# Keeping the scan rounds of a four-layer vision network in their written order on each engine

## The chip, the cores and the metric

The kernel runs on one core of one Trainium2 chip. The metric is the device time of one execution in microseconds, the median of several. A profile of one execution stands beside it; its span, from the first instruction to the last, is a little shorter than the device time (13,481.9 us against 13,525.9 us here).

The engines are called by the names of the profile: PE (TensorE, matmuls), PEld (its weight loads), DVE (VectorE), ACT (ScalarE), POOL (GpSimd) and SP (SyncE, which issues nearly all DMAs here). Each takes its own instructions from a queue.

## What is computed

The input is four images of 56 x 56 positions with 96 channels. Layers 0 and 1 are state-space blocks: normalisation, a projection to 192 inner channels, a selective scan over the 3136 positions in four directions (rows, rows reversed, columns, columns reversed), a gate, an output projection; layer 0 adds a two-matrix feed-forward stage, layer 1 convolutions, a fusion and a normalisation. Layers 2 and 3 are linear attention and a feed-forward stage quantised to 8-bit floats. Most of the work is the selective scan, for each image, direction, channel `d` and each of 16 states `n`:

```
dt = softplus(dt_raw @ dtw + dtb)
step:  h[d, n] = exp(dt[d] * A[d, n]) * h[d, n] + dt[d] * B[n] * u[d]
       y[d]    = sum over n of h[d, n] * C[n]
result y + u * D, the four directions added up
```

It is a recurrence along the positions, with 192 x 16 = 3072 independent rows per image and direction.

## The kernel before

**Tiling of the scan.** Each image and direction is cut into 7 chunks of 448 positions. Two layers, four images, four directions and 7 chunks give 224 chunks. A chunk is worked in 8 rounds, `r = 4 e + q`: `e` is the half of the channels (2 x 96), `q` one of four groups of four states. A round holds 3 groups `g` of 128 rows (32 channels x 4 states) by 448 positions. There are 1792 rounds, and `scans()` writes them one after the other, in a software pipeline laid out by hand.

**One round, n**, and the lines that make it:

- L475, PE: `b(n)`, the B values of the round spread over 128 rows, a matmul with a selection matrix into the one PSUM buffer `b`. It takes two instructions in the profile.
- L550, DVE: `v[:, g] = du * b` for g = 0, 1 (and 2 in rounds 5 and 6 of a chunk, the constant `OWN`).
- L522, POOL: in the other rounds `v[:, 2] = du * cb`, from a copy of B that a DMA has spread (`cb`). The code calls this `ahead`. The tile `v` has 3 buffers.
- L513, ACT: the decays `da = exp(dt * a)`, one for each g, into 3 PSUM buffers.
- L556, DVE: the scans, one for each g: `v` becomes the states h.
- L560, ACT: the last column is kept in `carry` for the next chunk of the same direction.
- L566, POOL: `hc = v * C` over all three groups (2 buffers).
- L581, PE, in `add_up`: the sum over the states, four matmuls (8 instructions) into the PSUM tile `y`. After the fourth round of a half, L590 or L592 adds `u * D` or the directions so far, and L593 (ACT) copies the sum into `Y`.

**Written order.** The loop over rounds writes: the products of L550 for round n; then `begin(n + 1)`, which holds `b(n + 1)` and POOL's product of L522 for n + 1; then the three scans of n, each followed by the decay of n + 1 for the same g; the carry copy; `hc` of n; and last `add_up` of n - 1. So on PE `b(n + 1)` is written ahead of the sum of n - 1, and on POOL the product of L522 for n + 1 is written ahead of `hc` of n.

**What feeds the rounds.** In rounds 3 to 7 and at round 0 of a chunk the loop also writes the preparation of the chunk that follows (of the second half at round 0): `project_step` (L413 on PE, L419 or L421 on ACT give `cf`; a DMA writes it to memory as `cd`), `step_sizes` (L433 on PE, softplus L436 on ACT gives `dtc`), `times_u` (L446 on POOL gives `duc`), `spread` (8 DMAs that fetch `dt` and `du`, spread over 128 rows, with 2 buffers each) and `fetch` (4 DMAs that fetch `cb` for one q, 6 buffers).

**The other stages.** At each step of the rounds' generator `tile_net` also draws steps from the stages of another image: `load`, `middle` (the end of layer 0 and the start of layer 1) or `tail` (the end of layer 1, layers 2 and 3), at a pace set by `lengths`. The last `tail` comes after the rounds. Their instructions, such as L620 and L614 (normalisation), L677 (convolution) and L823, go to the same queues.

**What sets the order.** The program isn't run in the order in which it is written. A scheduler plays it through with estimated durations, and on each engine takes the earliest-written instruction that is ready at that moment. The order it finds is the order of each engine's queue on the chip; the durations on the chip differ from its estimates. In the kernel before this holds for all instructions, the rounds' too.

Of the kernel before, what the change touches and what calls it, by code (L numbers as in the profile page):

```python
# [15 lines left out]
AF = mybir.ActivationFunctionType  # L16
ALU = mybir.AluOpType
# [5 lines left out]
C = 96  # L23
# [3 lines left out]
NG = 3  # L27
# [5 lines left out]
CS = 448  # L33
# [121 lines left out]
class Net:  # L155
# [227 lines left out]
    def in_order(self, a, orient, lo, n):  # L383

        a = a.rearrange("p (h w) -> p w h" if orient else "p (h w) -> p h w", w=HS)
        return a[:, lo // HS : (lo + n) // HS, :]

    def project_step(self, ch):

        nc, sp = self.nc, self.sp  # L390
        l, i, k = ch.l, ch.i, ch.k
        if ch.first:
            for n in range(4):
                a = slice(n * L // 4, (n + 1) * L // 4)
                for e in range(NE):
                    nc.sync.dma_start(self.U[e][:, a], self.ud[i][C * e : C * e + C, a])
        if ch.step == 0:
            wd = sp.tile([128, WD], F32, name="wd")
            nc.sync.dma_start(wd, self.aps["wd"][l, k])
            a = NE * 128  # L400
            self.wx = wd[:C, :a].rearrange("p (e m) -> p e m", e=NE)
            self.wt = wd[:, a : a + C]
            a += C
            self.dtb = wd[:C, a : a + NE]
            na = sp.tile([128, NE, NQ, NG], F32, name="na")
            nc.scalar.activation(na.rearrange("p e q g -> p (e q g)"), wd[:, a + NE :], AF.Exp)
            nc.gpsimd.tensor_scalar_mul(na, na, -1.0)
            self.na = na
            self.carry = sp.tile([128, NE, NQ, NG], F32, name="carry")
        ch.na, ch.carry, ch.wt, ch.dtb = self.na, self.carry, self.wt, self.dtb  # L410
        ps = self.ps()[:, :CS]
        for e in range(NE):
            nc.tensor.matmul(  # L413
                ps.rearrange("p (a b) -> p a b", b=HS), self.wx[:, e],
                self.in_order(self.U[e], ch.orient, ch.c * CS, CS), start=e == 0, stop=e == NE - 1,
            )
        ch.cf = sp.tile([128, CS], F32, name="cf")
        if l == 0:
            nc.scalar.activation(ch.cf, ps, AF.Copy, scale=self.cscale[:, k : k + 1])  # L419
        else:  # L420
            nc.scalar.copy(ch.cf, ps)  # L421
        ch.cd = self.dram.tile([2 * NS, CS], F32, tag="cd", name="cd", bufs=3)
        nc.sync.dma_start(ch.cd, ch.cf[: 2 * NS])
# [48 lines left out]
    def spread_b(self, ch, q):  # L472

        ps = self.psum.tile([128, 512], F32, tag="b", name="b", bufs=1)[:, :CS]
        self.nc.tensor.matmul(ps, self.sel[:, q], ch.cf, start=True, stop=True)  # L475
        return ps

    def scans(self):

        nc, sp = self.nc, self.sp
        chunks = []
        for l in range(2):
            for i in range(NB):
                for n, (orient, rev) in enumerate(ORDER):
                    for step in range(NCS):
                        ch = Step()
                        ch.l, ch.i, ch.orient, ch.rev, ch.step = l, i, orient, rev, step  # L490
                        ch.k = 2 * orient + rev if l == 0 else orient + 2 * rev
                        ch.c = NCS - 1 - step if rev else step
                        ch.first = n == 0 and step == 0
                        ch.skip = n == 0
                        ch.last = n == 3 and step == NCS - 1
                        ch.dt, ch.du, ch.cb = [], [], []
                        chunks.append(ch)
        ch = chunks[0]
        self.project_step(ch)
        self.step_sizes(ch)  # L500
        self.times_u(ch, 0)
        self.spread(ch, 0)
        self.times_u(ch, 1)
        for q in range(3):
            self.fetch(ch, q)
        rounds = [(ch, e, q) for ch in chunks for e in range(NE) for q in range(NQ)]
        nexts = dict(zip(chunks, chunks[1:]))

        def decay(n, g):

            ch, e, q = rounds[n]
            da = self.psum.tile([128, 512], F32, tag="da", name="da", bufs=3)[:, :CS]
            nc.scalar.activation(da, ch.dt[e][:, g], AF.Exp, scale=ch.na[:, e, q, g : g + 1])  # L513
            return da

        def begin(n):
            ch, e, q = rounds[n]
            b = self.spread_b(ch, q)
            v = sp.tile([128, NG, CS], F32, name="v", bufs=3)
            ahead = NQ * e + q not in OWN  # L520
            if ahead:
                nc.gpsimd.tensor_tensor(v[:, 2], ch.du[e][:, 2], ch.cb[q][:, 1], ALU.mult)  # L522
            return b, v, ahead

        nxt = begin(0)
        das = [decay(0, g) for g in range(NG)]
        late = None
        for n, (ch, e, q) in enumerate(rounds):
            r = NQ * e + q
            follow = nexts.get(ch)  # L530
            if r == 0:
                self.spread(ch, 1)
                self.fetch(ch, 3)
            if follow is not None:
                if r == 3:
                    self.project_step(follow)
                elif r == 4:
                    self.step_sizes(follow)
                    self.times_u(follow, 0)
                elif r == 5:  # L540
                    self.spread(follow, 0)
                    self.times_u(follow, 1)
                if r > 4:
                    self.fetch(follow, r - 5)
            way = slice(None, None, -1) if ch.rev else slice(None)
            end = 0 if ch.rev else CS - 1
            b, v, ahead = nxt
            at = ch.carry[:, e, q]
            for g in range(2 if ahead else 3):
                nc.vector.tensor_tensor(v[:, g], ch.du[e][:, g], b, ALU.mult)  # L550
            more = n + 1 < len(rounds)
            if more:
                nxt = begin(n + 1)
            for g in range(NG):
                da, das[g] = das[g], None
                nc.vector.tensor_tensor_scan(  # L556
                    v[:, g, way], da[:, way], v[:, g, way], at[:, g : g + 1] if ch.step else 0.0, ALU.mult, ALU.add
                )
                if g == 2 and ch.step < NCS - 1:
                    nc.scalar.copy(at.unsqueeze(2), v[:, :, end : end + 1])  # L560
                if more:
                    das[g] = decay(n + 1, g)
                if g < 2:
                    yield ch
            hc = sp.tile([128, NG, CS], F32, name="hc")
            nc.gpsimd.tensor_tensor(hc, v, ch.cb[q][:, 0].unsqueeze(1).to_broadcast([128, NG, CS]), ALU.mult)  # L566
            if late is not None:
                self.add_up(*late)
            late = (ch, e, q, hc)
            yield ch  # L570
        self.add_up(*late)
        yield None

    def add_up(self, ch, e, q, hc):

        nc = self.nc
        if q == 0:
            self.y = self.psum.tile([128, 512], F32, tag="y", name="y", bufs=1)[:, :CS]

        for n, g in enumerate((0, 1, 2, 2)):  # L580
            nc.tensor.matmul(  # L581
                self.y[32 * n : 32 * n + 32], self.four, hc[:, g], start=q == 0 or n == 3, stop=n == 3,
            )
        if q < NQ - 1:
            return
        y = self.in_order(self.Y[e], ch.orient, ch.c * CS, CS)
        o = self.y[:C].rearrange("p (a b) -> p a b", b=HS)
        if ch.skip:
            u = self.in_order(self.U[e], ch.orient, ch.c * CS, CS)
            nc.tensor.matmul(o, self.skip[ch.l][:, e], u, start=False, stop=True)  # L590
        else:
            nc.tensor.matmul(o, self.ident[:C, :C], y, start=False, stop=True)  # L592
        nc.scalar.copy(y, o)  # L593
        if ch.last:
            nc.sync.dma_start(self.yd[ch.i][C * e : C * e + C], self.Y[e])

# [428 lines left out]
```

## Time and profile before

| | before |
|---|---|
| device time, median of 3 (lowest to highest) | 13,525.92 us (13,524.19 to 13,527.72) |
| span of the profiled execution | 13,481.9 us |
| mean granted TensorE clock | 0.686 |
| end of the last scan | 12,879 us after the start |
| L556 scans on DVE | 5376, 5836.6 us busy |
| L550 products on DVE | 4032, 2329.5 us busy |
| L566 `hc` on POOL | 1792, 5427.9 us busy |
| L522 products on POOL | 1344, 1514.0 us busy |
| L513 decays on ACT | 5376, 3351.7 us busy |

The page gives busy time of each engine, then groups of instructions with the idle time before them and what ended it. An entry such as "DVE v L556 <- POOL v L522" in the list of waits reads: DVE stood idle ahead of an instruction of line 556 that writes `v`, until POOL's instruction of line 522 had ended; then the total in us, the number of waits and the longest. The timeline lists start and duration in us, engine, line, operation, tiles (out<-in), shapes and a count of merged instructions; the bracket at the end is the idle time of the engine just before, and what ended it.

### The profile page before, as it was taken

What the parts mean: (1) busy time and instruction counts of PE and PEld (TensorE: products, weight loads), DVE (VectorE), ACT (ScalarE), POOL (GpSimd) and SP (SyncE); (2) the same over time, 40 slices, a digit from 0 to 9 for tenths busy, and PEclk for the clock granted to TensorE, in tenths of its full rate; (3) what the DMA queues carried; (4) which work ended last, traced back from release to release, by engine and by line L of the source; (5) the groups of instructions that cost most, each with busy time, mean ns of one, the idle gap of its engine ahead of it and who ended that gap; (6) DMA issues with size and microseconds to landing.
All of it is one profiled execution on the core that took longest, in us unless ns stands there. A gap on an engine that the chain in (4) does not pass through costs nothing. (4 is left out here: it accounts for less than half of the span.)

```text
span 13481.9 us, 111978 instructions
## 1 busy us (share of the span) xinstructions
PE 9753.7 (72%) x30078; PEld 3150.5 (23%) x30078; DVE 8491.7 (63%) x10556; ACT 6039.2 (45%) x10401; POOL 7754.4 (58%) x3960
## 2 busy tenths in 40 slices
PE   6677677776777777776777777776777777777776
PEld 2221122211222122211222132211322212222133
DVE  4666766667666766667666655677556675566722
ACT  4544455444544455444554433344333453343511
POOL 4666665666666665666666645557545575555720
PEclk6766666766767676777767676666766667666665
DMA  4444444445444444445444433344334444343410
GB/s 120 118 111 118 117 118 112 111 108 129 115 107 113 116 119 110 112 109 132 115 108 108 114 94 93 90 107 122 95 82 99 96 120 100 89 97 88 118 45 26
DMA packets 940544, 1415.74 MB, mean 105 GB/s; under 512 B 175042, under 2 KB 926148, under 8 KB 938276
## 3 DMA queue, kind: packets, MB, share of 16 engines
q1 hardware_dynamic: 939136, 1406.79, 42.6%
q8 instruction: 237, 3.88, 0.1%
q14 instruction: 399, 3.27, 0.1%
q10 hardware_dynamic: 772, 1.80, 0.0%
HBM read 1139.85 MB, written 268.14 MB: 104 GB/s over the span
## 5 line engine op out<-in xcount | busy, mean ns | idle before, releaser
L566 POOL TENSOR_TENSOR hc<-v,cb 128x1344 f32<-128x1344 f32 x1792 | 5427.9, 3029 | 3097.5 <-DVE v L556 2569.8
L556 DVE TENSOR_TENSOR_SCAN v<-da,carry,v 128x448 f32<-128x448 f32 x4608 | 5042.5, 1134 | 1093.6 <-POOL v L522 821.5
L513 ACT ACTIVATE da<-dt,na 128x448 f32<-128x448 f32 x5376 | 3351.7, 634 | 1959.4 <-DVE v L556 1940.3
L581 PE MATMUL y<-hc,four 128*32 128x448 f32 x14336 | 2848.2, 776 | 1678.3 <-POOL hc L566 1663.9
L475 PE MATMUL b<-cf,sel 128*128 128x448 f32 x3584 | 2673.7, 841 | 1296.7 <-DVE v L550 1294.1
L550 DVE TENSOR_TENSOR v<-du,b 128x448 f32<-128x448 f32 x4032 | 2329.5, 605 | 1640.2 <-PE b L475 1463.7
L522 POOL TENSOR_TENSOR v<-du,cb 128x448 f32<-128x448 f32 x1344 | 1514.0, 1134 | 116.4 <-DMA cb<-cd 77.7
L475 PEld LDWEIGHTS b<-cf,sel 128*128 128x128 f32 x3584 | 830.3, 270 | 3079.5 <-DVE v L550 2464.0
L581 PEld LDWEIGHTS y<-hc,four 128*32 128x32 f32 x14336 | 374.1, 126 | 3756.3 <-POOL hc L566 3089.2
L446 POOL TENSOR_TENSOR duc<-dtc,U 96x448 f32<-96x448 f32 x448 | 552.5, 1244 | 1152.2 <-ACT dtc L436 1090.7
L560 ACT COPY carry<-v 128x3 f32<-128x3 f32 x1536 | 296.4, 193 | 1553.7 <-DVE v L556 1551.0
L593 ACT COPY Y<-y 96x448 f32<-96x448 f32 x448 | 340.0, 759 | 1442.0 <-PE y L592 1104.1
L617 POOL TENSOR_TENSOR rs<-rs,power 112x4 f32<-112x4 f32 x252 | 256.9, 1020 | 1248.3 <-ACT rs L616 1110.7
L556 DVE TENSOR_TENSOR_SCAN v<-da,v 128x448 f32<-128x448 f32 x768 | 794.1, 1073 | 176.5 <-POOL v L522 116.7
L413 PE MATMUL ps<-U,wd 96*128 96x448 f32 x896 | 667.9, 873 | 1.0 <-ACT h L877 0.9
L620 PE MATMUL ps<-ident,rs 112*96 112x112 f32 x2016 | 395.0, 364 | 317.0 <-POOL rs L617 316.7
L592 PE MATMUL y<-Y,ident 96*96 96x448 f32 x672 | 603.1, 990 | 0.0
L677 PE MATMUL ps<-win,dg 64*64 64x220 f32 (+10 forms) x2016 | 591.2, 491 | 0.0
L513 ACT ACT_TABLE_LOAD x432 | 554.3, 1283 | 10.5 <-DMA dt<-dd 3.3
L436 ACT ACT_TABLE_LOAD x313 | 401.6, 1283 | 174.5 <-PE ps L433 100.2
L620 PEld LDWEIGHTS ps<-ident,rs 112*96 112x96 f32 x2016 | 332.1, 242 | 458.2 <-POOL rs L617 435.3
L614 PEld LDWEIGHTS ps<-avg,w 96*112 96x112 f32 (+1 forms) x2240 | 354.6, 232 | 221.8 <-issue 95.3
(207 smaller groups left out, 5804.7 us busy)
## 6 DMA issues: line engine op xcount, KB each, us to landing
cb<-cd SPq DMA_DIRECT2D x3584, 112.0 KB, 3.9
dt<-dd SPq DMA_DIRECT2D x1792, 168.0 KB, 3.5
du<-dd SPq DMA_DIRECT2D x1792, 168.0 KB, 4.4
dd<-dtc SPq DMA_DIRECT2D x448, 168.0 KB, 2.1
dd<-duc SPq DMA_DIRECT2D x448, 168.0 KB, 2.2
U<-u SPq DMA_DIRECT2D x64, 294.0 KB, 6.2
y<-Y SPq DMA_DIRECT2D x16, 1176.0 KB, 6.6
u<-w SPq DMA_DIRECT2D x56, 224.0 KB, 2.8
```

Of the source, the lines that this page charges most:

```text
L413: nc.tensor.matmul(ps.rearrange("p (a b) -> p a b", b=HS), self.wx[:, e], self.in_order(self.U[e], ch.orient, ch.c * CS, CS), start=e == 0 ...
L446: nc.gpsimd.tensor_tensor(du.rearrange("p (a b) -> p a b", b=HS), ch.dtc[e].rearrange("p (a b) -> p a b", b=HS), self.in_order(self.U[e], ...
L475: self.nc.tensor.matmul(ps, self.sel[:, q], ch.cf, start=True, stop=True)
L513: nc.scalar.activation(da, ch.dt[e][:, g], AF.Exp, scale=ch.na[:, e, q, g : g + 1])
L522: nc.gpsimd.tensor_tensor(v[:, 2], ch.du[e][:, 2], ch.cb[q][:, 1], ALU.mult)
L550: nc.vector.tensor_tensor(v[:, g], ch.du[e][:, g], b, ALU.mult)
L556: nc.vector.tensor_tensor_scan(v[:, g, way], da[:, way], v[:, g, way], at[:, g : g + 1] if ch.step else 0.0, ALU.mult, ALU.add)
L566: nc.gpsimd.tensor_tensor(hc, v, ch.cb[q][:, 0].unsqueeze(1).to_broadcast([128, NG, CS]), ALU.mult)
L581: nc.tensor.matmul(self.y[32 * n : 32 * n + 32], self.four, hc[:, g], start=q == 0 or n == 3, stop=n == 3,)
L592: nc.tensor.matmul(o, self.ident[:C, :C], y, start=False, stop=True)
L620: nc.tensor.matmul(ps[:, b], rs[:, q : q + 1].to_broadcast([NT, C]), self.ident[:NT, :NT], start=True, stop=True)
L677: self.nc.tensor.matmul(o[:, a - r0 : e - r0, x0:x1], diag[:, tap], win[:, a + dy - lo : e + dy - lo, x0 + dx : x1 + dx], start=n == 0, st ...
```

## The change

Every instruction of the rounds gets a common mark. Among the instructions that carry it, the scheduler keeps the written order on each engine. Unmarked instructions (the preparation of the next chunk, the DMAs, the other stages) can still be placed anywhere between them. It is meant to make the chip follow the pipeline as it was laid out by hand, where the scheduler's estimates had led it to another order. No operation is added or removed; one operand of L566 is given a name on the way.

```diff
+    def keep(self, i):
+
+        self.tc.stamp_issue_order_token(i.ins, "rounds")
+
...
-        self.nc.tensor.matmul(ps, self.sel[:, q], ch.cf, start=True, stop=True)
+        self.keep(self.nc.tensor.matmul(ps, self.sel[:, q], ch.cf, start=True, stop=True))
...
-            nc.scalar.activation(da, ch.dt[e][:, g], AF.Exp, scale=ch.na[:, e, q, g : g + 1])
+            self.keep(nc.scalar.activation(da, ch.dt[e][:, g], AF.Exp, scale=ch.na[:, e, q, g : g + 1]))
...
-                nc.gpsimd.tensor_tensor(v[:, 2], ch.du[e][:, 2], ch.cb[q][:, 1], ALU.mult)
+                self.keep(nc.gpsimd.tensor_tensor(v[:, 2], ch.du[e][:, 2], ch.cb[q][:, 1], ALU.mult))
...
-                nc.vector.tensor_tensor(v[:, g], ch.du[e][:, g], b, ALU.mult)
+                self.keep(nc.vector.tensor_tensor(v[:, g], ch.du[e][:, g], b, ALU.mult))
...
-                nc.vector.tensor_tensor_scan(
+                self.keep(nc.vector.tensor_tensor_scan(
                     v[:, g, way], da[:, way], v[:, g, way], at[:, g : g + 1] if ch.step else 0.0, ALU.mult, ALU.add
-                )
+                ))
...
-                    nc.scalar.copy(at.unsqueeze(2), v[:, :, end : end + 1])
+                    self.keep(nc.scalar.copy(at.unsqueeze(2), v[:, :, end : end + 1]))
...
-            nc.gpsimd.tensor_tensor(hc, v, ch.cb[q][:, 0].unsqueeze(1).to_broadcast([128, NG, CS]), ALU.mult)
+            c = ch.cb[q][:, 0].unsqueeze(1).to_broadcast([128, NG, CS])
+            self.keep(nc.gpsimd.tensor_tensor(hc, v, c, ALU.mult))
...
-            nc.tensor.matmul(
+            self.keep(nc.tensor.matmul(
                 self.y[32 * n : 32 * n + 32], self.four, hc[:, g], start=q == 0 or n == 3, stop=n == 3,
-            )
+            ))
...
-            nc.tensor.matmul(o, self.skip[ch.l][:, e], u, start=False, stop=True)
+            self.keep(nc.tensor.matmul(o, self.skip[ch.l][:, e], u, start=False, stop=True))
         else:
-            nc.tensor.matmul(o, self.ident[:C, :C], y, start=False, stop=True)
-        nc.scalar.copy(y, o)
+            self.keep(nc.tensor.matmul(o, self.ident[:C, :C], y, start=False, stop=True))
+        self.keep(nc.scalar.copy(y, o))
```

## The prediction

> **What bounds the kernel now.** Part 1 of the page comes first: no engine is full, so waits set the time.
>
> ```profile
> PE 9753.7 (72%) x30078; PEld 3150.5 (23%) x30078; DVE 8491.7 (63%) x10556; ACT 6039.2 (45%) x10401; POOL 7754.4 (58%) x3960
> ```
>
> PE's figure covers modelled, overlapping matmuls. Of the others DVE has most to do, and the rounds give it nearly all of it: lines 550 and 556 (both forms) are 2329.5 + 5042.5 + 794.1 = 8166 us. The scans are serial on DVE, so I ask what ends DVE's idle 13,482 − 8,492 = 4,990 us. The list of waits names two large causes:
>
> ```profile
> DVE v L550 <- PE b L475: 1463.7, 474, 15.1
> DVE v L556 <- POOL v L522: 938.2, 609, 12.0
> ```
>
> I then split DVE's waits by place in the chunk: the k-th scan of line 556 belongs to round k div 3, and likewise for the other lines. Write T for the products of line 550, S for the scans, v2 for POOL's product of line 522, r0 to r7 for the rounds of a chunk. The 938 us lie in r0 to r3. Of the 1,464 us, 807 are T of r1 (164 waits, 4.92 us each) and 215 T of r7 (173 waits, 1.24 each). The other stages' instructions on DVE wait 2,067 us (493 of it after 12,879 us, when no round is left).
>
> The timeline shows how the first cause works, in a stretch without other stages (r1 to r2):
>
> ```profile
> 4592.60 0.59 DVE L550 TENSOR_TENSOR v<-du,b 128x448 f32<-128x448 f32 x1
> 4592.82 3.03 POOL L566 TENSOR_TENSOR hc<-v,cb 128x1344 f32<-128x1344 f32 x1 [1.33 <-DVE v L556]
> 4593.11 2.18 DVE L556 TENSOR_TENSOR_SCAN v<-da,carry,v 128x448 f32<-128x448 f32 x2
> 4593.24 1.86 PE L475 MATMUL b<-cf,sel 128*128 128x448 f32 x2 [1.07 <-DVE v L550]
> 4595.21 0.59 DVE L550 TENSOR_TENSOR v<-du,b 128x448 f32<-128x448 f32 x1
> 4595.81 1.14 POOL L522 TENSOR_TENSOR v<-du,cb 128x448 f32<-128x448 f32 x1
> 4595.90 1.72 PE L581 MATMUL y<-hc,four 128*32 128x448 f32 x8 [0.80 <-POOL hc L566]
> 4596.98 1.15 DVE L556 TENSOR_TENSOR_SCAN v<-da,carry,v 128x448 f32<-128x448 f32 x1 [1.18 <-POOL v L522]
> ```
>
> POOL runs hc of the round before (3.03 us) and only then v2, which this round's third scan needs: DVE stands 1.18 us and POOL then 1.33, so the two take turns. The period is 5.45 us (4596.98 − 4591.53, the same scan a round earlier). A round that waits for nothing takes 4622.94 − 4618.73 = 4.21 us:
>
> ```profile
> 4618.73 1.15 DVE L550 TENSOR_TENSOR v<-du,b 128x448 f32<-128x448 f32 x2 [1.91 <-PE b L475]
> 4619.80 3.23 DVE L556 TENSOR_TENSOR_SCAN v<-da,carry,v 128x448 f32<-128x448 f32 x3
> ...
> 4622.94 1.13 DVE L550 TENSOR_TENSOR v<-du,b 128x448 f32<-128x448 f32 x2
> ```
>
> The second cause, at the start of the same chunk (r0 to r1):
>
> ```profile
> 4576.97 1.72 PE L581 MATMUL y<-hc,four 128*32 128x448 f32 x8
> 4578.62 1.94 PE L592 MATMUL y<-Y,ident 96*96 96x448 f32 x2
> 4580.39 1.28 PE L475 MATMUL b<-cf,sel 128*128 128x448 f32 x2
> 4580.60 0.99 ACT L593 COPY Y<-y 96x448 f32<-96x448 f32 x1 [4.91 <-PE y L592]
> 4581.77 0.62 DVE L550 TENSOR_TENSOR v<-du,b 128x448 f32<-128x448 f32 x1 [4.77 <-PE b L475]
> 4583.61 1.34 POOL L446 TENSOR_TENSOR duc<-dtc,U 96x448 f32<-96x448 f32 x1 [6.21 <-ACT dtc L436]
> 4584.92 1.13 POOL L522 TENSOR_TENSOR v<-du,cb 128x448 f32<-128x448 f32 x1
> 4586.08 1.15 DVE L556 TENSOR_TENSOR_SCAN v<-da,carry,v 128x448 f32<-128x448 f32 x1 [3.69 <-POOL v L522]
> ```
>
> b of r1 stands on PE behind the old chunk's last sum and its identity matmul; ACT holds the new chunk's decays behind that sum's copy; POOL holds v2 of r0 behind duc of the next chunk, which waits for ACT. DVE loses 4.77 + 3.69 us.
>
> **What the Trainium skill says.** "PSUM — Partial Sum Buffer", Engine vs sequencer instructions: the queues of ScalarE, VectorE and GpSimd are strict FIFO, and matmuls start in program order. The trace agrees: v2 waited with its inputs there while duc, ahead of it, stood 6.21 us. "SBUF — State Buffer", Who interferes with whom: a DVE instruction with at most one SBUF input doesn't contend with GpSimd. T reads b from PSUM, S reads da from PSUM, and T takes 582 to 623 ns in all 4,032 cases, whatever POOL does; so running v2 beside other scans costs nothing. "TensorE: Matmul & The Clock Gate", What's actually happening: PE runs at half clock unless it has been busy. The trace shows 0.50 from 4586 to 4604 us and 0.75 from 4623 to 4800. I price PE at half clock.
>
> **The change, part by part.** No operation, buffer or byte is added or removed; only positions in the queues. From the order in the trace I count where before departs from the written order:
> - POOL: v2 starts after the preceding round's hc in 884 of 895 cases of r0 to r3, in none of r4 and r7. Written, v2(n+1) precedes hc(n).
> - PE: b of r1 follows y of r7 in 223 of 223 chunks, b of r7 follows y of r5 in 184. Written, b(n+1) precedes y(n−1).
> - DVE: T(n) slips before the last scan of n−1 in 820 cases, filling the wait for v2. ACT: the copy of Y runs ahead of decays written before it.
>
> New steady state, with S2(n−1) ending at 0. DVE: T to 1.1, scans to 4.2. PE: b(n+1) from 1.2 to 3.1 (1.86 us), then y(n−1), whose hc ends at about 3.2, until 4.9; b(n+2) is wanted at 5.4, so y delays nothing. POOL: hc(n−1) 0.1 to 3.2, v2(n+1) to 4.3, hc(n) at 4.3: 4.17 of work in 4.21. ACT: three decays, 3 × 0.64, each when a scan frees its buffer. So DVE sets 4.21 us, with POOL almost level. The new wait is hc behind v2: if cb or du lands late, hc and y stand too, but the third scan needs that v2 anyway, and in most chunks du and cb land one to three rounds ahead (the median issue of dt is 4 rounds ahead).
>
> The sums, all on DVE's path:
> - A, third scan for v2: 925 us. Of the 672 rounds r1 to r3, 520 take 5.3 to 5.6 us, so 520 × (5.45 − 4.21) = 645 is nearly sure; the rest hangs on r0 and on duc, which stays free to stand ahead of v2, now with a round's slack.
> - B, T of r1 for b: 807 us. b(r1) can start when T of r0 is done; the other stages' matmuls may still stand ahead.
> - C, T of r7 for b: 215 us.
> Together 1,947 us, or 8.7 per chunk. Left as they are: the other T waits for b (1,464 − 807 − 215 = 442, mostly behind convolution matmuls), S for decays (332), du (146), the other stages (2,067).
>
> How much is kept depends on what else a chunk holds. I count 50 chunks without other-stage work (47.8 us each, DVE idle 12.1), 56 with such matmuls alone (52.5, idle 17.3), 118 with other-stage DVE instructions (62.8, idle 23.8, of which 12.5 is these waiting for PE, ACT and POOL). In the first I take 8.5 us, in the second 8. In the last I take half, 4.5: a DVE that comes sooner to an instruction waiting for PE waits there longer. The bounds of that share are 0 and 8.7. Sum: 50 × 8.5 + 56 × 8 + 118 × 4.5 = 1,404; 13,526 − 1,404 = **12,120 us**.
>
> **The rivals.**
> - Only the steady part comes (A's 645): r0 stays held by duc, softplus and other matmuls, which have no order of their own. 12,880 us. For it: PE work sits ahead of b in most chunks. Against: the quiet chunk above stalls with hardly any.
> - More comes: all 1,947, S of r0 for decays (246 of the 332) and half of the 442, since Y's copy no longer blocks ACT. 13,526 − 2,414 = 11,110. Against: the other stages' waits must not grow.
> - Slower: b(n+1), waiting for DVE, now stands ahead of y and of all other-stage matmuls placed behind it; DVE's other-stage instructions wait for those matmuls. They wait 2,067 − 493 = 1,574 us within the scans; if that doubles while only 645 is won, 13,526 + 1,574 − 645 = 14,455; at +65% (1,020), 13,900, which I take. For it: the scheduler had moved these instructions for some reason, and its places for the other stages shift. Against: r4 to r6 mostly keep the written order on POOL and PE and run without these stalls.
> - No change, 13,526: gains eaten exactly.
>
> **How the numbers follow.** Forecast 0.50, steady part alone 0.20, more 0.14, slower 0.13, no change 0.03. Faster is 0.50 + 0.20 + 0.14 = 0.84. The range reaches from the larger gain, 11,100, past the smaller one to 13,200 (that case with the waits of the other stages 20% longer, 315 us); slower and no change stay out, 0.16.
>
> **What would show it.** A: hardly any wait of line 556 for line 522, steady rounds of about 4.2 us. B and C: line 550's wait for b below 600 us, b right behind T in r0. DVE at 69 to 71% of the span with the same busy time. The forecast falls if waits of lines 620, 823 or 834 on DVE grow past 3,000 us, if the wait for v2 remains (duc still ahead), or if line 566 waits for DMA.

## The result, and the profile after

The changed kernel takes 11,818.43 us (median of 4 runs, 11,805.97 to 11,857.94) against 13,525.06 us: a ratio of 0.8744 (95% interval 0.8722 to 0.8766), or 1,707 us less. Adding `keep` shifted the lines: 475 is now 479 (b), 513 is 517 (decays), 522 is 526 (POOL's third product, v2), 550 is 554 (T), 556 is 560 (scans), 566 is 571 (hc), 581 is 586 (the sum y), 592 is 597 (identity).

The busy times of the profile after, part 1 of its page:

```profile
PE 8717.8 (74%) x30078; PEld 2954.7 (25%) x30078; DVE 8442.5 (71%) x10556; ACT 6046.5 (51%) x10428; POOL 7740.7 (65%) x3960
```

DVE, ACT and POOL are busy for nearly the same time as before (ACT has 27 table loads more); the span is 1,626 us shorter (11,856.3), so their shares rise. PE's busy time falls by 1,036 us with the same instructions; more on that at the end. The two waits, from the list of waits:

```profile
DVE v L554 <- PE b L479: 653.3, 277, 11.2
DVE v L560 <- POOL v L526: 534.6, 113, 21.4
```

The first lost more than half, the second somewhat less. Round 3 of a chunk in the timeline after, from its third product on POOL to the products of round 4. In the timelines here, lines of ACT, PEld and DMA are left out, and `...` stands for the other gaps:

```profile
3984.98 1.15 POOL L526 TENSOR_TENSOR v<-du,cb 128x448 f32<-128x448 f32 x1
...
3986.23 1.13 DVE L554 TENSOR_TENSOR v<-du,b 128x448 f32<-128x448 f32 x2
3986.46 3.03 POOL L571 TENSOR_TENSOR hc<-v,cb 128x1344 f32<-128x1344 f32 x1 [0.34 <-DVE v L560]
3987.28 3.23 DVE L560 TENSOR_TENSOR_SCAN v<-da,carry,v 128x448 f32<-128x448 f32 x3
...
3989.44 1.16 POOL L526 TENSOR_TENSOR v<-du,cb 128x448 f32<-128x448 f32 x1
3989.55 1.72 PE L586 MATMUL y<-hc,four 128*32 128x448 f32 x8 [1.11 <-POOL hc L571]
3990.42 1.12 DVE L554 TENSOR_TENSOR v<-du,b 128x448 f32<-128x448 f32 x2
```

The third product of this round ran at 3984.98, ahead of hc of the round before (3986.46), so the three scans run together (3.23 us) and no bracket stands at DVE. The product that starts at 3989.44 is already that of round 4. The round takes 3990.42 − 3986.23 = 4.19 us. A window over rounds 2 to 5 of this chunk shows a full DVE; the columns are the window, its length, and busy time with the number of instructions of each engine, then PE's granted clock, the DMA share and GB/s:

```profile
3982.00:3999.00 17.00, 12.42 (x50) 2.78 (x50) 16.98 (x21) 8.81 (x18) 14.33 (x7) 0.79 0.62 139
```

About half of what is left of the two waits (362 us in round 0 and 224 us in round 2, of 1,188) arises near the start of a chunk:

```profile
3971.42 1.35 POOL L450 TENSOR_TENSOR duc<-dtc,U 96x448 f32<-96x448 f32 x1 [3.40 <-ACT dtc L440]
3972.73 1.13 POOL L526 TENSOR_TENSOR v<-du,cb 128x448 f32<-128x448 f32 x1
3973.81 3.03 POOL L571 TENSOR_TENSOR hc<-v,cb 128x1344 f32<-128x1344 f32 x1
3973.89 1.15 DVE L560 TENSOR_TENSOR_SCAN v<-da,carry,v 128x448 f32<-128x448 f32 x1 [3.03 <-POOL v L526]
...
3976.89 1.72 PE L586 MATMUL y<-hc,four 128*32 128x448 f32 x8 [6.22 <-POOL hc L571]
...
3978.55 1.94 PE L597 MATMUL y<-Y,ident 96*96 96x448 f32 x2
3980.31 1.68 PE L479 MATMUL b<-cf,sel 128*128 128x448 f32 x2
...
3982.02 1.15 DVE L554 TENSOR_TENSOR v<-du,b 128x448 f32<-128x448 f32 x2 [2.79 <-PE b L479]
```

duc of the next chunk, which carries no mark, stands on POOL ahead of v2 of round 0 and waits there for ACT. That costs DVE 3.03 us. Then hc of the old chunk's last round (3973.81) is late too, so are its sum (3976.89) and identity matmul, and b of round 2, now written behind that sum, costs another 2.79 us.

Placing DVE's idle time by round, as in the prediction, gives this table (us, counted in the traces; e1, e2, e7, e9 and e10 are the experiments below). It leaves out the scans' waits for decays, the waits of T for du, and the time after the last scan.

| DVE idle ahead of | before | after | e1 | e2 | e9 | e10 | e7 |
|---|---|---|---|---|---|---|---|
| third scan for v2, rounds 1 to 3 | 733 | 172 | 114 | 678 | 825 | 164 | 59 |
| third scan for v2, round 0 | 193 | 362 | 248 | 187 | 438 | 364 | 68 |
| T of round 1 for b | 807 | 43 | 164 | 218 | 49 | 1,188 | 171 |
| T of round 7 for b | 215 | 18 | 271 | 24 | 15 | 310 | 60 |
| T of round 2 for b | 50 | 224 | 307 | 60 | 16 | 0 | 67 |
| T of the other rounds for b | 392 | 368 | 451 | 421 | 232 | 353 | 386 |
| other stages, while rounds last | 1,580 | 1,332 | 1,345 | 1,388 | 1,435 | 1,278 | 1,314 |

Idle time fell by 1,577 us in all (4,985 to 3,409), which with 49 us less busy is the 1,626 of the span.

### The profile page after: what moved, and what is told of

Read it like the earlier page. It is cut to its first block, busy times and chain, and to the rows that moved or that the text cites. A ratio compares the mean times of both kernels' runs of the same rounds, so it can differ in the third digit from the quotient of the medians.

```text
span 11856.3 us, 112012 instructions
## 1 busy us (share of the span) xinstructions
PE 8717.8 (74%) x30078; PEld 2954.7 (25%) x30078; DVE 8442.5 (71%) x10556; ACT 6046.5 (51%) x10428; POOL 7740.7 (65%) x3960
## 4 chain that ended last, share of the span: by engine, by line
PE 24%; DVE 19%; issue 17%; POOL 10%; DMA 7%; ACT 7%; SPq 3%; DVEq 0%; POOLq 0%; ACTq 0%
DVE v L560 13%; POOL hc L571 6%; DVE v L554 4%; PE y L586 4%; PE ps L682 3%; DMA cb<-cd 3%; PE b L479 3%; SPq L463 2%; PE ps L625 2%; PE ps L417 2%; ACT da L517 2%; PE y L597 2%; DMA du<-dd 2%; POOL v L526 2%; POOL rs L622 1%
## 5 line engine op out<-in xcount | busy, mean ns | idle before, releaser
L560 DVE TENSOR_TENSOR_SCAN v<-da,carry,v 128x448 f32<-128x448 f32 x4608 | 4990.3, 1132 | 720.5 <-POOL v L526 476.5
L586 PE MATMUL y<-hc,four 128*32 128x448 f32 x14336 | 2375.3, 712 | 1240.8 <-POOL hc L571 1193.1
L479 PE MATMUL b<-cf,sel 128*128 128x448 f32 x3584 | 2298.2, 731 | 992.1 <-DVE v L554 989.7
L554 DVE TENSOR_TENSOR v<-du,b 128x448 f32<-128x448 f32 x4032 | 2266.8, 607 | 758.2 <-PE b L479 653.3
L479 PEld LDWEIGHTS b<-cf,sel 128*128 128x128 f32 x3584 | 724.9, 235 | 2612.1 <-DVE v L554 2075.8
L586 PEld LDWEIGHTS y<-hc,four 128*32 128x32 f32 x14336 | 331.2, 121 | 2871.1 <-POOL hc L571 2478.8
L597 PE MATMUL y<-Y,ident 96*96 96x448 f32 x672 | 577.4, 950 | 0.0
```

What stands on the lines that cost most here:

```text
L479: self.keep(self.nc.tensor.matmul(ps, self.sel[:, q], ch.cf, start=True, stop=True))
L554: self.keep(nc.vector.tensor_tensor(v[:, g], ch.du[e][:, g], b, ALU.mult))
L560: self.keep(nc.vector.tensor_tensor_scan(v[:, g, way], da[:, way], v[:, g, way], at[:, g : g + 1] if ch.step else 0.0, ALU.mult, ALU.add))
L586: self.keep(nc.tensor.matmul(self.y[32 * n : 32 * n + 32], self.four, hc[:, g], start=q == 0 or n == 3, stop=n == 3,))
L597: self.keep(nc.tensor.matmul(o, self.ident[:C, :C], y, start=False, stop=True))
```

## The experiments

Ratios are to the kernel before on the same chip, with 95% intervals.

### Which engine's order matters: POOL alone, PE alone, both

The mark is given only on the engines named:

```diff
     def keep(self, i):
-        self.tc.stamp_issue_order_token(i.ins, "rounds")
+        if i.ins.engine in (mybir.EngineType.Pool, ):
+            self.tc.stamp_issue_order_token(i.ins, "rounds")
```

> Only the rounds' POOL instructions keep the written order (the product of line 526 ahead of the preceding round's hc). Theory (each queue's order costs by itself): the third scan's wait for that product in rounds 1 to 3 goes (733 us before), rounds 2 and 3 take about 4.2 us, the wait of T in round 1 for b (807 us) stays: 12,700 to 12,950 us. Rival 1 (the queues are coupled: one engine's order drags the others along): near the full change, 11,800 to 12,000, with the b waits gone too. Rival 2 (POOL's order alone only moves the wait elsewhere): 13,400 or more.

Measured: 12,323.9 us, 0.9116 (0.9099 to 0.9132), 1,198 us less; the theory's window began at 12,700. The waits of the third scan did fall as it said, to 114 us in rounds 1 to 3. But the wait of T in round 1 fell as well, from 807 to 164. The trace shows how: b of round 1 stands behind the old half's sum in 0 chunks here, in 223 before. A likely reason, not shown, is that with hc held behind v2 the scheduler saw the sum ready later and placed b first. So Rival 1 has a part in it: a mark on one queue moved another queue's order. It did not move all of it; b of round 7 is still behind the sum in 194 of 223 chunks (184 before), and T of round 7 waits 271 us for it.

With `mybir.EngineType.PE` in its place:

> Only the rounds' PE instructions keep the written order (b of the next round ahead of y of the round before). Theory (each queue by itself): the waits of T in rounds 1 and 7 for b (1,022 us before) fall below 150, the third scan's wait for POOL stays near 900 us, rounds 1 to 3 stay at 5.45 us: 12,500 to 12,750 us. Rival 1 (coupled): 11,800 to 12,000 with both waits gone. Rival 2 (b ahead of y makes PE stand for DVE, with the other stages behind): slower than before, above 13,600.

Measured: 12,421.1 us, 0.9188 (0.9174 to 0.9203), 1,100 us less. Here only PE changed: v2 still follows hc as before (215 to 223 of 223 chunks in each of rounds 0 to 3), rounds 1 to 3 stay near 5.45 us and the wait for v2 at 865 us in all. The waits of rounds 1 and 7 for b are 242 us together, short of the theory's 150 but 780 below before, and the time is 80 us better than its window. Rival 2, PE standing for DVE with the other stages behind it, falls: the other stages' waits on DVE went down, 1,580 to 1,388.

With both engines:

> POOL and PE keep the written order, DVE and ACT are free. Theory (POOL's and PE's orders are the whole cause; DVE's slipping of T ahead of the last scan was only a filler of the wait for POOL): within 1% of the full change, 11,750 to 11,950 us. Rival (the orders of DVE and ACT matter too, above all the copy of Y ahead of the decays on ACT): 12,100 us or more, with scans waiting for decays as before (332 us).

Measured: 11,930.6 us, 0.8829 (0.8813 to 0.8845). That is 112 us above the full change, just inside 1%, but their intervals lie apart, so the orders of DVE and ACT add something. POOL and PE carry 1,591 of the 1,707 us. Alone they gave 1,198 + 1,100 = 2,298, so they share about 700; e1's effect on b of round 1 is one overlap that the traces show.

### DVE and ACT

The mark is given on the other two engines alone:

> DVE and ACT keep the written order, POOL and PE are free. Theory (POOL's and PE's orders are the whole cause): both large waits stay, 13,300 to 13,650 us, possibly slower than before, since T no longer fills the wait for POOL. Rival (the orders of DVE and ACT carry the gain, or drag POOL and PE into the written order): 12,500 us or less.

Measured: 12,998.2 us, 0.9619 (0.9599 to 0.9638): 523 us less, where the theory had none. The next two runs take them apart: ACT alone (e5), DVE alone (e6).

> Only the rounds' ACT instructions (decays, carry copy, copy of Y) keep the written order. Theory (half of the previous run's unexpected gain of 523 us is ACT: the copy of Y no longer stands ahead of the next chunk's softplus and decays, so duc and with it v2 of round 0 come some 3 us sooner in each chunk): 12,950 to 13,100 us, the wait of T in round 1 for b near 300 us, rounds 2 and 3 still 5.45 us. Rival (the gain was DVE's strict order): 13,400 to 13,600.

Measured: 13,322.9 us, 0.9850 (0.9832 to 0.9869), 199 us less. The theory's mechanism fails: T of round 1 waits 830 us for b, as before. What fell most is the first scan of round 0 waiting for its decays, 246 to 123 us.

> Only the rounds' DVE instructions keep the written order. Theory (T's slipping ahead of the last scan only fills a wait): 13,450 to 13,700 us, no large change in any wait but T of round 1 moved behind the last scan. Rival (strict order on DVE brings the 523 us): 12,950 to 13,100.

Measured: 13,189.9 us, 0.9756 (0.9741 to 0.9770), 332 us less, against the theory. In the 50 chunks that hold no other stage it is right: they take 47.7 us, 47.8 before. The wait of T in round 1 for b only changes its place to the third scan of round 0, which now comes first: 807 + 193 = 1,000 us become 241 + 652 = 893. The chunks with other-stage work are about 1.6 to 1.8 us shorter each, and why is not settled: their instructions may have come to lie better, and PE's mean granted clock is 0.720 here, 0.686 before. In the 50 chunks the clock rose too (0.65 to 0.69) and did not make them shorter.

### Undoing one order inside the full change

All rounds' instructions stay marked; only the place at which one is written moves. First v2 of rounds 0 to 3, behind hc (`third` holds the product that `begin` wrote):

```diff
-            if ahead:
-                self.keep(nc.gpsimd.tensor_tensor(v[:, 2], ch.du[e][:, 2], ch.cb[q][:, 1], ALU.mult))
+            if ahead and (e == 1 or n == 0):
+                third(n, v)
...
             self.keep(nc.gpsimd.tensor_tensor(hc, v, c, ALU.mult))
+            if more and rounds[n + 1][1] == 0:
+                third(n + 1, nxt[1])
```

> All rounds' instructions marked as in the full change, but the third product (POOL) of rounds 0 to 3 is written behind hc of the round before, the order that the kernel before had. Theory (that one inversion makes POOL and DVE take turns): rounds 1 to 3 go back to 5.45 us or a little more, the third scan's wait for POOL rises from 535 us to over 1,000, and the run takes (5.45 - 4.2) x 3 x 224 = 840 us more than the full change: 12,500 to 12,800 us. Rival (the gain in rounds 1 to 3 came from the other queues): within 2% of the full change, below 12,050.

Measured: 12,411.0 us, 0.9186 (0.9168 to 0.9204), 593 us above the full change. The taking of turns is back: the medians of rounds 1 to 3 are 5.46, 5.45 and 5.45 us, and 527 of the 672 take 5.3 to 5.6 us (5 in the full change, 520 before).

```profile
DVE v L564 <- POOL v L531: 1262.9, 735, 21.7
```

This is the wait of the third scan in e9's list of waits, 1,263 us against 535. The time is less than the 840 us I worked out, and below the window. One reason is that the full change pays elsewhere for its order: with hc first, the old half's sum is done sooner, and T of round 2 waits 16 us for b instead of 224, T of the rounds 3 to 6 and 0 waits 232 instead of 368.

Then the sum ahead of b in rounds 1 and 7; the copy of Y, which belongs to the same call, moves ahead with it:

```diff
+            if late is not None and r in (0, 6):
+                self.add_up(*late)
+                late = None
             if more:
                 nxt = begin(n + 1)
```

> All rounds' instructions marked as in the full change, but the sum of two rounds ago is written ahead of b in rounds 1 and 7 (and with it the copy of Y ahead of the decays of round 1), as the kernel before had it. Theory: T of round 1 waits for b again 3 to 4.5 us a chunk, T of round 7 about 1: 700 to 1,000 us on top of the full change, less the 224 us that round 2 waits there: 12,300 to 12,700 us. Rival (with the other orders kept the old half's sum is done in time, so b behind it costs nothing): below 12,000 us.

Measured: 12,932.3 us, 0.9567 (0.9551 to 0.9582), 1,114 us above the full change, more than the theory's window. The timeline of e10 at the start of a chunk (574 is hc, 589 the sum, 600 the identity matmul there):

```profile
4371.06 1.35 POOL L450 TENSOR_TENSOR duc<-dtc,U 96x448 f32<-96x448 f32 x1 [3.74 <-ACT dtc L440]
4372.37 1.12 POOL L526 TENSOR_TENSOR v<-du,cb 128x448 f32<-128x448 f32 x1
4373.46 3.01 POOL L574 TENSOR_TENSOR hc<-v,cb 128x1344 f32<-128x1344 f32 x1
...
4376.52 1.72 PE L589 MATMUL y<-hc,four 128*32 128x448 f32 x8 [8.55 <-POOL hc L574]
...
4378.18 1.94 PE L600 MATMUL y<-Y,ident 96*96 96x448 f32 x2
4379.94 1.63 PE L479 MATMUL b<-cf,sel 128*128 128x448 f32 x2
...
4381.61 1.15 DVE L554 TENSOR_TENSOR v<-du,b 128x448 f32<-128x448 f32 x2 [6.93 <-PE b L479]
```

PE stands 8.55 us for an hc that itself was held behind v2 and duc, and b waits behind it, so T of round 1 loses 6.93 us here. The two orders need each other: v2 ahead of hc makes hc late, and a late hc costs most where b is queued behind its sum.

### What duc still costs

The full change, with the product of line 450 marked as well:

```diff
-        nc.gpsimd.tensor_tensor(
+        self.keep(nc.gpsimd.tensor_tensor(
             du.rearrange("p (a b) -> p a b", b=HS),
...
             ALU.mult,
-        )
+        ))
```

> The full change, and POOL's product duc (line 450) of the next chunk keeps the written order too: after hc of rounds 3 and 4, not ahead of v2 of round 0. Theory (what is left of the third scan's wait in round 0, 362 us, and the new wait of T in round 2 for b, 224 us, come from duc standing on POOL for ACT's softplus): both fall below 100 us, POOL's wait for dtc (1,040 us) nearly vanishes, 11,250 to 11,500 us. Rival (duc then comes too late for the loads of du): T of round 0 waits for the DMA of du for over 400 us (103 us in the full change), 11,800 us or more.

Measured: 11,589.4 us, 0.8571 (0.8559 to 0.8584): the fastest of all, 229 us below the full change. The two waits in its list of waits, over all rounds, are these:

```profile
DVE v L554 <- PE b L479: 682.8, 250, 9.2
DVE v L560 <- POOL v L526: 126.8, 36, 16.8
```

Of them, 68 us are the third scan of round 0 and 67 us T of round 2, both below 100; du lands in time (74 us of waiting), and the chunks without other stages take 37.5 us with 2.8 us of idle DVE, against 40.9 with 5.8. It missed its window because other waits grew: T of round 1 for b by 128 us, scans for decays by 106, and POOL's wait for dtc is still 638 us. The median round 0 takes 4.62 us, 7.33 in the full change and 13.50 before.

> As the run before, and ACT's softplus (line 440) of the next chunk keeps the written order as well, in round 4 behind the decays. Theory (only duc's place matters, softplus ahead of time costs two table loads wherever it stands): within 1% of the run before. Rival 1 (with softplus at round 0 the decays of round 1 come late): faster by over 1%. Rival 2 (softplus just ahead of duc makes POOL wait in round 4, and du lands late): slower by over 1%, with T of round 0 waiting for du.

The edit wraps the softplus of line 440 in `self.keep` too. Measured: 11,727.2 us, 0.8682 (0.8666 to 0.8697), 138 us slower than e7. That is by over 1%, as in Rival 2, but not for its reason: du is waited for 64 us only. T of round 1 waits 422 us for b (171 in e7), and the first scan of round 5 waits 218 us for its decays, behind the softplus.

## Why the prediction was right, and where a size was off

**The mechanism held, engine by engine.** Forecast 12,120 us, range 11,100 to 13,200; measured 11,818. v2 starts behind the preceding hc in no case after (884 of 895 before), b behind the sum in no case. Rounds that wait for nothing take 4.19 us (4.21 forecast). DVE's share is 71%, as forecast; e9 and e10 undo one order each, and its waits come back. T and the scans take as long as before (584 to 623 ns, and 1,114 to 1,152 ns with a carry), so v2 beside the scans cost nothing, as assumed.

**A was too high.** I called 645 us nearly sure, from 520 rounds of 5.45 us. The third scan's wait in rounds 1 to 3 did lose 561 us, but these 520 rounds (each from the end of one last scan to the next) are only 366 us shorter in all, and 322 of them take 4.1 to 4.3 us. Where they are round 2 they gain nothing on average (5.44 to 5.43 us): T of round 2 waits 174 us more for b, and round 0 waits 169 us more for v2. What was off is "with a round's slack": duc stays ahead of v2 and waits for ACT long enough to use the slack up. I had named that as the sign to look for ("duc still ahead"). e7 shows it for round 0 and for round 2, which take 4.62 us (median) and 4.63 us (mean of the same rounds) there. But duc is not all of it: in e7 the 520 rounds are 407 us shorter, still not 645, since round 1 now waits more for b and for decays.

**B and C were right and nearly whole**: 961 of 1,022 us. The wait of line 554 for b fell to 653 us, somewhat above the 600 I set, because of round 2.

**The share kept in busy chunks was the mis-sized term.** For the same three groups of 50, 56 and 118 chunks as before, the chunks became 6.9, 7.8 and 7.2 us shorter (47.8 to 40.9, 52.5 to 44.7, 62.8 to 55.6); I had 8.5, 8 and 4.5. The sum 50 × 6.9 + 56 × 7.8 + 118 × 7.2 = 1,631 us is the span's gain. Two errors, of opposite sign: the quiet chunks kept less because of duc, and the halving for chunks with other-stage DVE work was wrong. Those instructions do not wait longer when the rounds come sooner; per chunk their idle time fell from 12.5 to 10.4 us. Of the 7.2 us, 2.1 are these waits and 5.1 the rounds' own, not far from the 4.5; what the sum left out is that the other stages gain as well. Whether that is PE's higher clock or better places in the queues was not tried.

**The rivals.** "Steady part alone" falls, since round 0 shrank from a median of 13.50 to 7.33 us. "Slower" falls, e2 above all: with b ahead the other stages wait less, not more. "No change" falls with the time. "More" was too large: ACT's order, of which the copy of Y is a part, is worth 199 us alone, and ACT and DVE together 112 on top of POOL and PE.

## What to carry to other kernels

Where a scheduler has placed instructions by estimated durations, list each engine's order against the order in which the pipeline was written, round by round; an instruction that is always one place late shows as two engines taking turns, and the period gives a first estimate of the cost (in e9, 840 us worked out from it and 593 measured). Put right all queues that take part in the loop together, since a correct order on one of them can make the next one's wrong order dearer (e10). Then look at what is not held in place: one unmarked instruction that waits for a third engine (duc) took back part of the gain, and holding it brought 229 us; holding its source as well (softplus) gave 138 of them back.

## What the hardware showed that I had not expected

PE got faster without a change to its work. Summed over the clock records of the trace, it runs at full clock for 4,977 us before and 6,059 us after, although the span is shorter; the mean granted clock goes from 0.686 to 0.757, and busy time from 9,754 to 8,718 us. I had priced PE at half clock throughout. Since DVE sets the pace in rounds without other work, this can only have helped where PE was waited for; how much of the gain it makes up was not separated. The experiments show that a higher clock alone does not remove the waits: e1 has nearly the clock of the full change (0.752) and takes about 500 us longer, and e10 has 0.733, well above before, yet T of round 1 waits 1,188 us for b, more than the 807 of before.
